# Selective scan: the read-out on TensorE one pair behind the scans instead of two, and the even step sizes issued at the end of the third pair

## The chip, the core and the metric

The kernel runs on one core of a Trainium2 chip. The metric is device time in microseconds (us) of one execution; the profile is one more execution, taken by the hardware profiler.

The core's engines work through their own instruction queues and meet at semaphores. The profile calls them PE (TensorE, matmuls; PEld are its weight loads), DVE (VectorE), ACT (ScalarE), POOL (GpSimd) and SP (SyncE). In this kernel SP issues all the DMAs that carry data.

## The reference

Two blocks run one after the other on an input of 16 images of 64 x 64 pixels with 96 channels. The first upsamples each image, passes it through a small network and downsamples it. The second holds the part that matters here, a selective scan along four directions over the 4096 pixels of an image, with 192 channels and 16 states for each direction:

```python
def selective_scan(u, dts, As, Bs, Cs, Ds, dt_bias):
    delta = jax.nn.softplus(dts + dt_bias[None, :, :, None])
    ...
    def step(h, inps):
        dt, ut, bt, ct = inps
        h = jnp.exp(dt[..., None] * As[None]) * h + (dt * ut)[..., None] * bt[:, :, None, :]
        y = jnp.einsum('bkdn,bkn->bkd', h, ct)
        return (h, y)
    _, ys = jax.lax.scan(step, h0, (dT, uT, BT, CT))
    ...
    return ys + u * Ds[None, :, :, None]
```

For each pixel the state `h` decays by `exp(delta * A)` and gains `delta * u * B`; the output `y` is the sum of `h * C` over the 16 states. Around this stand a normalization, an input projection, a depthwise convolution with silu, the projections that make `delta`, `B` and `C`, and an output projection.

## The kernel before

**Tiles.** A tile of the scan has 128 partitions: 32 channels times 4 states. A stretch of `T = 1024` pixels lies along the free axis. 16 states need four such tiles; the index `j` = 0 to 3 counts them. Two groups of 32 channels are taken together and are called the halves of a *pair*: the odd half, `e = 1`, and the even half, `e = 0`. Six blocks (`bi`) of two groups make up the 12 groups of 192 channels in two directions, and 128 steps (16 images, two direction pairs, four stretches) follow each other. So `units` lists 128 x 6 x 4 = 3072 pairs, numbered `n`, and `m = n // 4` counts the blocks.

**What a pair does.** `drive(n)` (L761, POOL) makes `delta * u * B` of both halves in one instruction, into a tile `b`. `decay(n, e)` (L755, ACT) makes `exp(delta * A)` of one half in PSUM, tile `da`. `recur(n, e)` (L770 forwards, L772 backwards, DVE) is the scan over the 1024 pixels; it overwrites `b` for the odd half and `da` for the even half (in every fifth pair `da` for both). The scan's result is multiplied by C: for the odd half on POOL (L917), for the even half on DVE (L927), both into `b`. In every fifth pair (`SHARE = 5`) the odd half's product is made on DVE too (L909). `keep` (L778) saves the last column of each scan for the next stretch. `read_out(n)` (L794, PE) sums the four states of each channel with eight matmuls (a quarter of the stretch of one half each) into the PSUM tile `y`, which gathers the four pairs of a block; for the second direction pair a matmul with `y0` (L787) opens the sum. `store` copies `y` out after a block's last pair (L805, ACT, tile `yt`) and sends it to HBM (L810 or L815, SP).

**Buffers.** There are four `b` tiles: `drive(n + 2)` writes where pair n - 2 was, so it waits for that pair's read-out. PSUM has two `da` tiles and one `y` tile. `delta` has three tiles in SBUF, each for one half of one block; `dtu`, the product of `delta` and `u`, has two. `bt` and `ct` have five tiles each.

**Order.** The order of the loop body is written by hand, and each engine keeps it. A pair n runs: fetches, odd scan, `keep`, `decay(n + 1, 1)`, `read_out(n - 2)`, slot 0, the odd product on POOL, `drive(n + 2)`, even scan, slot 1, even product, `keep`, `decay(n + 1, 0)`, slot 2, further fetches. The three *slots* are places where background work is put, a piece at a time: the projections of the next step (`project`, L655 to L696), the first block and convolution of the next image (`front`, L240 to L517) and the end of the last image (`finish`, L519 to L608). These share PE and ACT with the scan, and their pieces stand in the same queues.

**Fetches.** At `j == 0` SP issues the next block's `dtu`, at `j == 1` its odd `delta` and at `j == 3` its even `delta` (L703 issues all of them). `bt` and `ct` of the other direction are issued at the end of certain pairs (L722); in two of the six blocks that falls between pairs `j = 2` and `j = 3`. All of these carry 512 KB each.

Of the kernel before, what the change touches and what calls it, by code (L numbers as in the profile page):

```python
# [64 lines left out]
NQ = 4  # L65
# [14 lines left out]
def tile_two_blocks(  # L80
# [534 lines left out]
    def scan():  # L615


        with ExitStack() as es:
# [81 lines left out]
            def spread(out, what, ctx, bi, e):  # L700

                v, s0, r = blocks[bi]
                nc.sync.dma_start(  # L703
                    out=out,
                    in_=ctx[what][v][32 * (s0 + e):32 * (s0 + e) + 32, :].unsqueeze(1).to_broadcast([32, NQ, T]),
                )

            def fetch_dtu(ctx, bi):
                t = p2.tile([128, 2, T], F32, name="dtu")
                for e in range(2):  # L710
                    spread(t[:, e, :], "dtu", ctx, bi, e)
                return t

            def fetch_delta(ctx, bi, e):
                t = p3.tile([128, T], F32, name="delta")
                spread(t, "delta", ctx, bi, e)
                return t
# [16 lines left out]
            units = [(si_, bi, j) for si_ in range(len(steps)) for bi in range(len(blocks)) for j in range(NQ)]  # L734
# [7 lines left out]
            deltas = {(0, e): fetch_delta(ctxs[0], 0, e) for e in (1, 0)}  # L742
            y0s, states, ys = {}, [None] * len(blocks), {}

            def group(n, e):
                st, bi, _ = units[n]
                v, s0, r = blocks[bi]
                return 2 * steps[st][1] + r, s0 + e if v < 2 else 4 + e
# [3 lines left out]
            def decay(n, e):  # L752
                k, g = group(n, e)
                da = aps.tile([128, T], F32, name="da")
                nc.scalar.activation(da, deltas[n // NQ, e], AF.Exp, scale=a_s[:, k, g, units[n][2]:units[n][2] + 1])  # L755
                das[n, e] = da
# [23 lines left out]
            def read_out(n):  # L780
                st, bi, j = units[n]
                _, pair, lc = steps[st]
                if j == 0:
                    ys[n // NQ] = yps.tile([128, 2, QT], F32, name="y")
                y = ys[n // NQ]
                if j == 0 and pair == 1:
                    nc.tensor.matmul(  # L787
                        y.rearrange("p e t -> p (e t)"), lhsT=ident_s, rhs=y0s.pop((lc, bi)), start=True,
                        stop=False, skip_group_check=True,
                    )  # L790
                b = bs.pop(n)
                for e in range(2):
                    for q in range(NQ):
                        nc.tensor.matmul(  # L794
                            y[32 * q:32 * q + 32, e, :], lhsT=fold_s, rhs=b[:, e, QT * q:QT * q + QT],
                            start=(pair == 0 and j == 0 and e == 0), stop=(j == NQ - 1), skip_group_check=True,
                        )

            def store(n):

                st, bi, _ = units[n]
                mi, pair, lc = steps[st]
                v, s0, r = blocks[bi]
                yt = yp.tile([128, 2, QT], F32, name="yt")
                nc.scalar.copy(yt, ys.pop(n // NQ))  # L805
                yield
                if pair == 0:
                    part = dram.tile([128, 2 * QT], F32, name="part", tag=f"part{lc}_{bi}")
                    ypart[lc, bi] = part
                    nc.sync.dma_start(out=part, in_=yt.rearrange("p e t -> p (e t)"))  # L810
                else:
                    g = s0 if v < 2 else 4
                    for q in range(NQ):
                        first = T * lc + QT * q
                        nc.sync.dma_start(  # L815
                            out=image[mi]["y"][r, 32 * g:32 * g + 64, first:first + QT].rearrange(
                                "(e c) t -> c e t", e=2
                            ),
                            in_=yt[32 * q:32 * q + 32, :, :],
                        )  # L820

            class Background:
# [7 lines left out]
                def slot(self, position):  # L830
                    self.at += 1
                    if self.wait and position < 2:
                        return
                    if self.gen is not None and self.n * self.positions < self.at * self.slices:
                        self.step()
# [20 lines left out]
            last = len(units) - 1  # L856
# [13 lines left out]
            storing = None  # L870

            for n, (st, bi, j) in enumerate(units):
                mi, pair, lc = steps[st]
                v, s0, r = blocks[bi]
                m = n // NQ
                if n % per_image == 0:
                    image[mi]["y"] = dram.tile([2, DI, L], F32, name="y_d")
                    behind_gen.drain()
                    ahead_gen = behind_gen = nothing
                    if mi + 1 < B:  # L880
                        ahead_gen = Background(front(mi + 1), SLICES, POS)
                elif n % per_image == 2 and mi > 0:
                    behind_gen = Background(finish(mi - 1), SLICES, POS)
                if j == 0:
                    new = stp.tile([128, 2, NQ], F32, name="new", tag=f"st{bi}")
                    states[bi] = (states[bi][1] if states[bi] else None, new)

                if j == 0:
                    ahead = None
                    if bi + 1 < len(blocks):  # L890
                        ahead = ctxs[st], bi + 1
                    elif n + NQ <= last:
                        step_gen.drain()
                        ahead = ctxs[st + 1], 0
                        next_step(st + 2, mi)
                    if ahead:
                        dtus[m + 1] = fetch_dtu(*ahead)
                elif j == 1:
                    if ahead:
                        deltas[m + 1, 1] = fetch_delta(*ahead, 1)  # L900
                elif j == 3:
                    if ahead:
                        deltas[m + 1, 0] = fetch_delta(*ahead, 0)

                odd_here = n % SHARE == SHARE - 1
                h = das[n, 1] if odd_here else bs[n][:, 1, :]
                recur(n, 1, h)
                if odd_here:
                    nc.vector.tensor_mul(bs[n][:, 1, :], h, bc[1, r, j])  # L909
                keep(n, 1, h, nc.scalar.copy if odd_here else nc.vector.tensor_copy)  # L910
                if n < last:
                    decay(n + 1, 1)
                if n >= 2:
                    read_out(n - 2)
                slot(0)
                if not odd_here:
                    nc.gpsimd.tensor_mul(h, h, bc[1, r, j])  # L917
                if n + 2 <= last:
                    drive(n + 2)

                h = das[n, 0]
                recur(n, 0, h)
                if n >= 2 and units[n - 2][2] == NQ - 1:
                    storing = store(n - 2)
                    next(storing)
                slot(1)
                nc.vector.tensor_mul(bs[n][:, 0, :], h, bc[1, r, j])  # L927
                keep(n, 0, h, nc.scalar.copy)
                if n < last:
                    decay(n + 1, 0)  # L930
                slot(2)
                if storing is not None:
                    next(storing, 0)
                    storing = None
                if j == NQ - 1 and n < last and steps[units[n + 1][0]][1] == 1:
                    st2, bi2, _ = units[n + 1]
                    y0s[steps[st2][2], bi2] = fetch_y0(steps[st2][2], bi2)


                at = n % per_step  # L940
                for what in range(2):
                    ahead_j = at - (2 * NQ - 1 + what)
                    if 0 <= ahead_j < NQ:
                        bc[what, 1, ahead_j] = fetch_bc(ctxs[st], 1, ahead_j, what)
                    ahead_j = at - (5 * NQ - 1 + what)
                    if 0 <= ahead_j < NQ and st + 1 < len(steps):
                        bc[what, 0, ahead_j] = fetch_bc(ctxs[st + 1], 0, ahead_j, what)
            for n in (last - 1, last):
                read_out(n)
            for _ in store(last):  # L950
                pass
            behind_gen.drain()
# [109 lines left out]
```

## Time and profile before

| | us |
|---|---|
| median of 3 runs | 21647.74 |
| lowest and highest | 21629.93 and 21659.27 |
| the profiled execution | 21651.91 |
| its span, first to last instruction | 21650.1 |
| scan stage in it | 541 to 21488 |

A line of the groups gives: source line, engine, operation, tile written and read, shape, count, then busy time and mean duration of one in nanoseconds, then the idle time of the engine just before these instructions and what ended most of it. A line of the waits gives: who waited, for whom, us in total, number of times, longest. A timeline line gives the start in us, the length, engine, source line and operation, and in brackets the idle time before it.

The costliest instructions of the scan stage:

```profile
L761 POOL TENSOR_TENSOR b<-dtu,bt 128x2048 f32<-128x2048 f32 x3072 | 13898.6, 4531 | 1341.2 <-PE y L794 617.3
L755 ACT ACTIVATE da<-delta,a_s 128x1024 f32<-128x1024 f32 x6144 | 6845.6, 1116 | 3099.3 <-DVE b L770 795.3
L917 POOL TENSOR_TENSOR b<-b,ct 128x1024 f32<-128x1024 f32 x2458 | 5798.8, 2359 | 631.1 <-DVE new L778 291.2
L794 PE MATMUL y<-b,fold_s 128*32 128x256 f32 x49152 | 3623.5, 420 | 331.3 <-DVE b L927 141.1
L927 DVE TENSOR_TENSOR b<-da,ct 128x1024 f32<-128x1024 f32 x3072 | 3756.6, 1223 | 93.9
```

A scan takes about 2.3 us on DVE and there are two to a pair. Each fp32 matmul of the program stands in the trace as two.

### The profile page before, as it was taken

The page shows a single profiled execution, that of the slowest core. Times are in us where ns is not written, and L with a number is a line of the kernel's source. Part 1 is how long each engine was busy: PE and PEld are TensorE (multiplying, and loading weights), DVE is VectorE, ACT ScalarE, POOL GpSimd, SP SyncE. Part 2 cuts the span into 40 slices and gives each one's busy share as a digit, 9 for nine tenths or more (in the row PEclk, how much of TensorE's full clock was granted, in tenths as well). Part 3 has the DMA queues.
Part 4 walks back from the last instruction along what each step waited for, and adds up shares of the span by engine and source line. Part 5 has one row for each costly group of instructions (what it writes and reads, how often), then busy time and mean ns, then how long its engine had stood idle before and what let it go on. Part 6 is the DMA issues. An engine that isn't in the chain of part 4 may idle for free. (4 is left out here: it accounts for less than half of the span.)

```text
span 21650.1 us, 273738 instructions
## 1 busy us (share of the span) xinstructions
PE 16910.3 (78%) x98988; PEld 7341.1 (34%) x98988; DVE 19532.7 (90%) x12983; ACT 13726.8 (63%) x20546; POOL 19514.3 (90%) x5538
## 2 busy tenths in 40 slices
PE   7776877877778787887778788787787778877855
PEld 4423324233342333324333242333423333243221
DVE  0999999999999999999999999999999999999997
ACT  3666666666666666666666666676666666666553
POOL 0999999999999999999999999999999999999996
PEclk8887888988889888888888888888898888988977
DMA  2565565656656566565655656566565665656654
GB/s 71 182 206 183 201 220 185 222 188 204 217 184 224 185 216 200 191 226 180 219 194 201 221 183 215 192 204 213 191 226 182 214 201 193 225 181 219 216 188 141
DMA packets 1855467, 4277.13 MB, mean 198 GB/s; under 512 B 449438, under 2 KB 548670, under 8 KB 1852062
## 3 DMA queue, kind: packets, MB, share of 16 engines
q1 hardware_dynamic: 1854110, 4259.62, 59.0%
q8 instruction: 781, 12.80, 0.3%
q14 instruction: 576, 4.72, 0.1%
HBM read 3380.58 MB, written 878.18 MB: 197 GB/s over the span
## 5 line engine op out<-in xcount | busy, mean ns | idle before, releaser
L761 POOL TENSOR_TENSOR b<-dtu,bt 128x2048 f32<-128x2048 f32 x3072 | 13898.6, 4531 | 1341.2 <-PE y L794 617.3
L755 ACT ACTIVATE da<-delta,a_s 128x1024 f32<-128x1024 f32 x6144 | 6845.6, 1116 | 3099.3 <-DVE b L770 795.3
L917 POOL TENSOR_TENSOR b<-b,ct 128x1024 f32<-128x1024 f32 x2458 | 5798.8, 2359 | 631.1 <-DVE new L778 291.2
L794 PE MATMUL y<-b,fold_s 128*32 128x256 f32 x49152 | 3623.5, 420 | 331.3 <-DVE b L927 141.1
L927 DVE TENSOR_TENSOR b<-da,ct 128x1024 f32<-128x1024 f32 x3072 | 3756.6, 1223 | 93.9
L770 DVE TENSOR_TENSOR_SCAN da<-da,new,b 128x1024 f32<-128x1024 f32 x1383 | 3247.0, 2348 | 386.8 <-ACT da L755 361.7
L772 DVE TENSOR_TENSOR_SCAN da<-da,new,b 128x1024 f32<-128x1024 f32 x1382 | 3242.8, 2346 | 230.3 <-ACT da L755 212.4
L794 PEld LDWEIGHTS y<-b,fold_s 128*32 128x32 f32 x49152 | 1386.6, 117 | 2917.1 <-issue 1271.0
L686 PE MATMUL s<-w,ident_s 128*128 128x512 f32 x1536 | 1212.9, 882 | 1345.3 <-ACT w L681 1265.6
L772 DVE TENSOR_TENSOR_SCAN b<-da,new,b 128x1024 f32<-128x1024 f32 x922 | 2157.9, 2340 | 45.9 <-ACT da L755 36.3
L770 DVE TENSOR_TENSOR_SCAN b<-da,new,b 128x1024 f32<-128x1024 f32 x921 | 2156.3, 2341 | 13.3 <-ACT da L755 8.5
L778 ACT COPY new<-da 128x1 f32<-128x1 f32 x2764 | 434.6, 157 | 2723.5 <-DVE b L927 2195.3
L482 PE MATMUL c_ps<-xgp,wtap_s 96*128 96x512 f32 (+1 forms) x4608 | 1694.3, 635 | 163.2 <-ACT row L500 158.7
L666 PE MATMUL s<-pr,dtw_s 128*128 128x512 f32 x1536 | 1005.9, 741 | 1000.2 <-ACT pr L659 495.9
L365 PE MATMUL h_ps<-xu,w1t_s 96*128 96x500 f32 x1920 | 1044.0, 644 | 293.7 <-ACT hsq L348 120.6
L377 PE MATMUL o_ps<-w2c_s,hsq 128*100 128x96 f32 x9600 | 1061.3, 270 | 187.0 <-ACT hsq L348 161.8
L772 DVE TENSOR_TENSOR_SCAN da<-da,b 128x1024 f32<-128x1024 f32 x461 | 1055.9, 2291 | 120.4 <-ACT da L755 120.0
L770 DVE TENSOR_TENSOR_SCAN da<-da,b 128x1024 f32<-128x1024 f32 x460 | 1053.7, 2291 | 121.0 <-ACT da L755 116.5
L655 PE MATMUL pp<-u,xpt_s 128*128 128x512 f32 x1536 | 922.1, 741 | 305.7 <-DMA u<-xs_d 205.0
L377 PEld LDWEIGHTS o_ps<-w2c_s,hsq 128*100 128x100 f32 x9600 | 992.2, 182 | 393.0 <-ACT hsq L348 218.9
L686 PE MATMUL s<-e,ident_s 128*128 128x512 f32 x1536 | 1088.3, 800 | 0.0
L482 PEld LDWEIGHTS c_ps<-xgp,wtap_s 96*128 96x128 f32 (+1 forms) x4608 | 611.5, 173 | 1113.8 <-issue 896.3
(128 smaller groups left out, 21643.8 us busy)
## 6 DMA issues: line engine op xcount, KB each, us to landing
dtu<-dtu_d SPq DMA_DIRECT2D x1536, 512.0 KB
delta<-delta_d SPq DMA_DIRECT2D x1536, 512.0 KB
bt<-rows SPq DMA_DIRECT2D x1024, 512.0 KB
ct<-rows SPq DMA_DIRECT2D x1024, 512.0 KB
u<-xs_d SPq DMA_DIRECT2D x896, 256.0 KB
dtu_d<-dtu SPq DMA_DIRECT2D x768, 256.0 KB
delta_d<-delta SPq DMA_DIRECT2D x768, 256.0 KB
xr<-in_x SPq DMA_DIRECT2D x768, 128.0 KB
```

Of the source, the lines that this page charges most:

```text
L365: nc.tensor.matmul(h_ps[j], lhsT=w1t_s[:, 128 * j:128 * (j + 1)], rhs=xu.rearrange("c p q -> c (p q)"), start=True, stop=True,)
L377: nc.tensor.matmul(o_ps[:, p, :], lhsT=hsq[j][:, UPS * p:UPS * (p + 1)], rhs=w2c_s[:, j, :], start=(j == 0), stop=(j == HB - 1),)
L482: nc.tensor.matmul(c_ps[p:p + n], lhsT=wtap_s[:, tap, 128 * i:128 * i + n], rhs=xgp[:, h0:h0 + 8, dx:dx + HW], start=(tap == 0), stop=(tap ...
L666: nc.tensor.matmul(s, lhsT=dtw_s[:, pair, v, :], rhs=pr, start=True, stop=True)
L686: nc.tensor.matmul(s, lhsT=ident_s, rhs=of, start=(k == 0), stop=(k == 3))
L755: nc.scalar.activation(da, deltas[n // NQ, e], AF.Exp, scale=a_s[:, k, g, units[n][2]:units[n][2] + 1])
L761: nc.gpsimd.tensor_mul(b, dtus[n // NQ], bt.unsqueeze(1).to_broadcast([128, 2, T]))
L770: nc.vector.tensor_tensor_scan(out, da, b, before, ALU.mult, ALU.add)
L772: nc.vector.tensor_tensor_scan(out[:, ::-1], da[:, ::-1], b[:, ::-1], before, ALU.mult, ALU.add)
L794: nc.tensor.matmul(y[32 * q:32 * q + 32, e, :], lhsT=fold_s, rhs=b[:, e, QT * q:QT * q + QT], start=(pair == 0 and j == 0 and e == 0), sto ...
L917: nc.gpsimd.tensor_mul(h, h, bc[1, r, j])
L927: nc.vector.tensor_mul(bs[n][:, 0, :], h, bc[1, r, j])
```

## The change

It moves three things in the loop body, and nothing else:

```diff
-                elif j == 3:
-                    if ahead:
-                        deltas[m + 1, 0] = fetch_delta(*ahead, 0)
...
-                if n >= 2:
-                    read_out(n - 2)
                 slot(0)
+                if storing is not None:
+                    next(storing, 0)
+                    storing = None
...
                 recur(n, 0, h)
-                if n >= 2 and units[n - 2][2] == NQ - 1:
-                    storing = store(n - 2)
-                    next(storing)
+                if n >= 1:
+                    read_out(n - 1)
                 slot(1)
...
                     decay(n + 1, 0)
+                if n >= 1 and units[n - 1][2] == NQ - 1:
+                    storing = store(n - 1)
+                    next(storing)
                 slot(2)
-                if storing is not None:
-                    next(storing, 0)
-                    storing = None
+                if j == 2 and ahead:
+                    deltas[m + 1, 0] = fetch_delta(*ahead, 0)
...
-            for n in (last - 1, last):
-                read_out(n)
+            read_out(last)
```

The read-out of pair n - 1 now stands in pair n, behind the even scan and between slots 0 and 1; before, that of pair n - 2 stood in pair n ahead of slot 0. The first half of `store`, the copy of `y` on ACT, moves from between the even scan and slot 1 of the pair with `j = 1` to behind the even decay of the pair with `j = 0`. Its second half, the DMA, moves from behind slot 2 to behind slot 0, in the pair with `j = 1`. The even `delta` of the next block is issued behind slot 2 of pair `j = 2`, ahead of any `bt` and `ct` that are issued there, instead of at the start of pair `j = 3`. As two lines fall away above them, L909, L917 and L927 become L906, L915 and L924 in the changed program.

## What the change does to the time

> **What bounds the kernel now.** I read the page's busy shares first, then the busy time by stretch, the groups of VectorE by line with what ended their idle time, the waits of GpSimd, and the timeline at three stalls.
>
> ```profile
> PE 16910.3 (78%) x98988; PEld 7341.1 (34%) x98988; DVE 19532.7 (90%) x12983; ACT 13726.8 (63%) x20546; POOL 19514.3 (90%) x5538
> ...
> 541.00:21488.00 20947.00, 16368.15 (x96398) 7060.03 (x96398) 19504.72 (x12916) 13490.84 (x20168) 19511.11 (x5530) 0.86 0.60 202
> ```
>
> The second line is the scan stage: 20947 us for 3072 pairs, 6.82 us each. VectorE (DVE) works 19505 us of it and GpSimd (POOL) 19511 us, so both are near their floor and about 1440 us of idle time on each is all that a new order can win. Which wait ends last on DVE is told by its groups (busy, mean ns, idle before, releasers):
>
> ```profile
> L770 DVE TENSOR_TENSOR_SCAN da<-da,new,b 128x1024 f32<-128x1024 f32 x1383 | 3247.0, 2348 | 386.8 <-ACT da L755 361.7 <-POOL b L761 23.9
> L772 DVE TENSOR_TENSOR_SCAN da<-da,new,b 128x1024 f32<-128x1024 f32 x1382 | 3242.8, 2346 | 230.3 <-ACT da L755 212.4 <-POOL b L761 17.2
> ...
> L691 DVE TENSOR_TENSOR dtu<-s,u 128x512 f32<-128x512 f32 x768 | 523.5, 682 | 362.3 <-PE s L686 352.9 <-DMA out<-o 5.7 <-DMA dtu<-dtu_d 2.4
> ```
>
> Over all eight scan groups the decays of ACT (L755) end 993 us of DVE's idle time, GpSimd's drive (L761) only 58.6 us. L691 waits for TensorE 353 us, of which 156 (124 waits) lie in the scan stage. GpSimd's own waits look different:
>
> ```profile
> POOL b L761 <- PE y L794: 617.3, 365, 8.3
> ...
> POOL b L917 <- DVE new L778: 291.2, 224, 12.2
> ```
>
> 365 times a drive stands still until a read-out (L794) has released a `b` buffer. One such place, PE and then POOL:
>
> ```profile
> 11828.58 8.36 PE L482 MATMUL c_ps<-xgp,wtap_s 96*128 96x512 f32 x12 [4.66 <-ACT row L500]
> 11836.77 1.02 PE L686 MATMUL s<-w,ident_s 128*128 128x512 f32 x2
> ...
> 11841.16 1.07 PE L794 MATMUL y<-b,fold_s 128*32 128x256 f32 x16
> ```
>
> ```profile
> 11842.34 4.53 POOL L761 TENSOR_TENSOR b<-dtu,bt 128x2048 f32<-128x2048 f32 x1 [5.63 <-PE y L794]
> ```
>
> The read-out, 1.07 us of work whose data were ready, stands behind background matmuls of the pair before, and GpSimd idles 5.63 us. The two kinds of decay that make DVE wait are these:
>
> ```profile
> 10823.66 1.12 ACT L755 ACTIVATE da<-delta,a_s 128x1024 f32<-128x1024 f32 x1 [1.55 <-DVE b L772]
> ...
> 10824.81 2.36 DVE L772 TENSOR_TENSOR_SCAN da<-da,new,b 128x1024 f32<-128x1024 f32 x1 [1.00 <-ACT da L755]
> ```
>
> ```profile
> 8016.51 2.15 ACT L755 ACTIVATE da<-delta,a_s 128x1024 f32<-128x1024 f32 x2 [5.77 <-DMA delta<-delta_d]
> ```
>
> In the first, the even decay of a pair could start only when the odd scan of the same pair had emptied its PSUM tile; DVE then stands for 1.00 us. In the second, an even step size (`delta`) had not landed.
>
> **What the Trainium skill says.** "PSUM — Partial Sum Buffer", section "Engine vs sequencer instructions": ACT, VectorE and GpSimd take their queues strictly in order, and matmuls start and complete in program order. The timeline at 11836 agrees: a ready read-out waited for L686. "Perfetto Trace Analysis", section "Optimization Strategy": the same gap coming back can mean that the next tile finds no room in SBUF or PSUM; the 1.00 us gaps before even scans are of that kind. "DMA: Bandwidth & Descriptors", section "Queues, rings and completion order": a DMA engine takes its descriptors in ring order, so a transfer issued behind two others pays for them; the 5.77 us wait agrees. "SBUF — State Buffer", section "Who interferes with whom", has VectorE and GpSimd share a port pair as an exclusive lock; here L761 stays within 4482 to 4638 ns and L927 within 1199 to 1228, so I charge nothing when GpSimd's instructions shift in time.
>
> **The change part by part.** No instruction is added or removed, and the orders on DVE and POOL are the same in both programs, line by line. Only PE, ACT and SP queues are rearranged.
>
> *Read-out.* On PE the 8 matmuls of pair n-1 move ahead of the background of slots 1 and 2 of pair n and behind that of slot 0; on average they pass 5 matmuls. Going through the trace pair by pair, I took the end of the last matmul that stays ahead, added 1.1 us, and set it against the end of GpSimd's instruction before the drive that needs the buffer: of some 620 us of stalls about 12 us are left. The data are no obstacle: the odd half's product (L917) ended a median 3.3 us, and at the 99th percentile 0.0 us, before the even scan of the next pair began, and L927 at least 2.2 us before. So the GpSimd wait goes. Its worth for the end is not 617 us but what DVE lost: 58.6 us. Bounds 0 and -100 (scans set free may also let ACT go sooner); I take -55.
>
> *What is late next on PE.* One read-out more now lies in front of the work of slots 1 and 2. Where PE runs without a break that work comes 1.07 us later, and slot 0's as much sooner. L691 waits 124 times for L686 in the stage; some three fifths of these L686 groups lie in slots 1 and 2. Taking 75 x 1.07 = +80 us, less about 45 for the rest, gives +35; bounds -60 and 124 x 1.07 = +130. ACT's waits for PE (L310 378 us, L348 261 us as the largest) shift in the same way; as decays have about 1 us (even) or 2.4 us (odd) to spare, I take +20, bounds -20 and +100. PE itself waits for younger data in some pairs, but in 2404 pairs with passed work the first passed matmul would be later by 1611 us in sum, of which only 286 exceed the read-out's own 1.1 us.
>
> *Store.* The copy of `yt` (L805, 574 ns, 768 times) moves from in front of ACT's keep and even decay to behind that decay, where the next deadline is the odd decay's, with more room. It would find its read-out unfinished in 64 of 768 cases, 103 us in all, against 28.9 now. I take +15, bounds -40 and +75. Its DMA is issued about two slots sooner on SP; nothing there waits for it. TensorE's wait for `yt` before a block's first read-out is 846 us now and lies on PE's slack.
>
> *Even step sizes.* On SP the issue stays where it was in four of six blocks: end of pair 2 and start of pair 3 are the same place in the queue. In the two where `bt` and `ct` are fetched there, it passes both. ACT waits 369 us for `delta`; without the first load it is 127 waits and 280 us, all on the even half of a block's first pair, and 110 of them (231 us) in exactly those two blocks. DVE stood 138 us behind all, 111 us behind those. The issues take 0.65 us each, and 1 MB at 202 GB/s for a 0.60 share, so 337 GB/s at full share, is an estimated 3.1 us: up to 4.4 us sooner, against late times of up to 5.8. I take -85, bounds -20 (the ring was not the cause) and -111. `bt` and `ct` are later by one transfer and are needed two pairs afterwards.
>
> *PSUM tiles of the decay.* Which of the two tiles a decay gets depends on the order in which the program was laid out. By the semaphores, the even decay waits for the odd scan of its own pair in 550 pairs before and in 472 after (94 lost, 16 new). The 94 cost DVE 76 us in this trace; -76 + 16 x 1.0 = -60, bounds -80 and 0.
>
> Sum: -55 + 35 + 20 + 15 - 85 - 60 = -130 us. The profiled execution took 21651.9 us (span 21650.1), 4 us above the median of the runs. 21651.9 - 130 - 4 = 21518; I say 21520 us, 0.6% less.
>
> **The rivals.**
> - *GpSimd is the true bound* and its 617 us come back as time. For it: 90% busy, and in four of five pairs its 4.53 + 2.36 us exceed DVE's 5.9. Against: DVE waited for it 58.6 us only. Half of 617 with the other terms: 21651.9 - 4 - 309 - 75 = 21265, say 21300.
> - *Hidden or given back*: the decays of ACT stay the last wait, and what DVE gains it stands elsewhere. For it: 472 PSUM waits remain. Nearly all of -130 is lost: 21640.
> - *Slower*: PE in order. The read-out waits for a pair just finished, and the background behind it (projection, convolution) reaches ACT and DVE late. Price: the 1611 us of later matmul starts; from the point at which more than 200 us of that (one eighth) come through to scans, the gains are used up. At one fifth, 322 us: 21648 - 200 + 322 = 21770. Against: ACT reaches that work only after the odd scan and a decay, 2.34 + 1.12 = 3.5 us after L927.
> - *The fetch does nothing*, as the text of the change promises a pair and the queue shows two DMAs: 21520 + 85 = 21605; inside the forecast's own range.
>
> **How the numbers follow.** Forecast 0.64 (own range 21400 to 21604), GpSimd bound 0.12, hidden 0.12, slower 0.12. With all bounds good or bad the sum runs from -411 to +285 us; all at once is unlikely, so the range is 21370 to 21660, which leaves out most of the slow rival and of the GpSimd one. About 0.2%, 43 us, is what a measurement of this kernel can tell from no change: faster 0.76, same 0.12, slower 0.12.
>
> **What would show it.** GpSimd's L761 waits for PE below 60 us; DVE's for POOL below 15; ACT's waits for `delta` below 120 us; ACT's decays still ending some 850 us of DVE's idle time; L691's wait for L686 up by tens of us. I am wrong if the time falls by more than 250 us (then GpSimd was bound), or if L691, `row` or `hsq` wait hundreds of us more for TensorE.

## The result, and the profile after

| | before | after |
|---|---|---|
| median, us | 21646.94 | 21501.44 |
| lowest to highest | 21629.93 to 21659.27 | 21488.61 to 21508.85 |
| span of the profiled execution | 21650.1 | 21507.1 |
| scan stage in it | 543.0 to 21488.3 | 536.2 to 21343.3 |

The ratio is 0.9924, 95% interval 0.9912 to 0.9936: 145 us less. The scan stage gives 138 us of the span's 143. The scan stage is counted here from the first scan to the last product. The page's busy shares and the busy time of the scan stage (PE, PEld, DVE, ACT, POOL) show that no engine's work went away; the same work lies closer together:

```profile
PE 16918.9 (79%) x98988; PEld 7271.3 (34%) x98988; DVE 19512.2 (91%) x12983; ACT 13741.5 (64%) x20546; POOL 19511.8 (91%) x5538
...
536.00:21344.00 20808.00, 16384.12 (x96406) 6995.77 (x96410) 19484.51 (x12916) 13503.65 (x20167) 19506.86 (x5530) 0.86 0.60 203
```

The groups of VectorE, with what ended its idle time, answer to the three lines shown before:

```profile
L770 DVE TENSOR_TENSOR_SCAN da<-da,new,b 128x1024 f32<-128x1024 f32 x1383 | 3246.5, 2347 | 282.8 <-ACT da L755 274.7 <-POOL b L761 6.9
L772 DVE TENSOR_TENSOR_SCAN da<-da,new,b 128x1024 f32<-128x1024 f32 x1382 | 3242.4, 2346 | 125.5 <-ACT da L755 119.1 <-POOL b L761 5.2
...
L691 DVE TENSOR_TENSOR dtu<-s,u 128x512 f32<-128x512 f32 x768 | 523.5, 682 | 431.9 <-PE s L686 430.6 <-DMA delta<-delta_d 0.8
```

The two largest groups lost 209 us of idle time, and L691's wait for TensorE grew by 78 us. Over all eight scan groups the waits for GpSimd fell from 58.6 to 22.7 us. GpSimd's own waits, and ACT's for `delta` without the program's first load (350 us in 140 waits before):

```profile
POOL b L915 <- DVE new L778: 832.6, 438, 16.0
...
POOL b L761 <- PE y L794: 47.9, 25, 5.3
```

```profile
ACT da L755 <- DMA delta<-delta_d: 60.3, 19, 4.5
```

GpSimd hardly waits for read-outs any more (617.3 us before); it waits for VectorE instead (291.2 us before). Its idle time mostly changed hands: in the scan stage it shrank from 1436 us to 1301, no more than the stage did. The place that stalled it in the timeline of before looks like this after, first TensorE, then VectorE, then GpSimd:

```profile
11756.75 1.07 PE L794 MATMUL y<-b,fold_s 128*32 128x256 f32 x16
11757.75 2.84 PE L482 MATMUL c_ps<-xgp,wtap_s 96*128 96x512 f32 x6
11760.43 1.02 PE L686 MATMUL s<-w,ident_s 128*128 128x512 f32 x2
```

```profile
11764.06 0.69 DVE L691 TENSOR_TENSOR dtu<-s,u 128x512 f32<-128x512 f32 x1 [3.55 <-PE s L686]
```

```profile
11758.43 4.51 POOL L761 TENSOR_TENSOR b<-dtu,bt 128x2048 f32<-128x2048 f32 x1
```

In the trace of before the same L691 stood like this:

```profile
11840.41 0.69 DVE L691 TENSOR_TENSOR dtu<-s,u 128x512 f32<-128x512 f32 x1 [1.42 <-PE s L686]
```

The read-out now precedes the background, and the drive starts without a wait (5.63 us before). The background pays: L691, which waited 1.42 us there, waits 3.55.

To see the whole of it I went through VectorE's instructions in both traces, and put each idle stretch over 0.05 us in the scan stage down to the operand that came last. An even decay counts as "own tile" when the program makes it wait for the odd scan of its own pair (in every fifth pair for the product that follows it). The first row has those that began within 0.15 us of that release, 435 before and 419 after. The second has 101 and 58 whose tile had been free for longer when ACT, busy with other work, came to them; the tile did not hold these up. The rows are good to some 3 us.

| VectorE idle, us | before | after | two tags, before (E3) | two tags, after (E4) |
|---|---|---|---|---|
| even decay, own tile, begun at its release | 392 | 378 | 0 | 0 |
| even decay, own tile, but ACT later still | 165 | 82 | 0 | 0 |
| even decay, `delta` not landed | 139 | 38 | 187 | 34 |
| even decay, late otherwise | 38 | 23 | 224 | 136 |
| odd decay late | 209 | 304 | 184 | 223 |
| L691 for TensorE | 160 | 232 | 176 | 157 |
| drive (GpSimd) | 56 | 16 | 66 | 24 |

So the even decays that ACT made late, whatever their tile (second and fourth row), cost 203 us before and 105 after, while the tile itself cost nearly as much as before.

### The profile page after: what moved, and what is told of

Its sections match the earlier page's. It is cut to its first block, busy times and chain, and to the rows that moved or that the text cites. A ratio compares the mean times of both kernels' runs of the same rounds, so it can differ in the third digit from the quotient of the medians.

```text
span 21507.1 us, 273615 instructions
## 1 busy us (share of the span) xinstructions
PE 16918.9 (79%) x98988; PEld 7271.3 (34%) x98988; DVE 19512.2 (91%) x12983; ACT 13741.5 (64%) x20546; POOL 19511.8 (91%) x5538
## 5 line engine op out<-in xcount | busy, mean ns | idle before, releaser
L915 POOL TENSOR_TENSOR b<-b,ct 128x1024 f32<-128x1024 f32 x2458 | 5804.1, 2361 | 1235.6 <-DVE new L778 832.6
L794 PE MATMUL y<-b,fold_s 128*32 128x256 f32 x49152 | 3837.1, 435 | 1111.6 <-DVE b L924 551.4
L924 DVE TENSOR_TENSOR b<-da,ct 128x1024 f32<-128x1024 f32 x3072 | 3756.5, 1223 | 93.9
L666 PE MATMUL s<-pr,dtw_s 128*128 128x512 f32 x1536 | 939.0, 696 | 544.6 <-ACT delta L692 328.0
L686 PE MATMUL s<-e,ident_s 128*128 128x512 f32 x1536 | 1022.9, 755 | 0.0
L787 PE MATMUL y<-y,ident_s 128*128 128x512 f32 x768 | 534.1, 784 | 538.6 <-ACT yt L805 537.1
```

Source lines behind the costliest of these rows:

```text
L666: nc.tensor.matmul(s, lhsT=dtw_s[:, pair, v, :], rhs=pr, start=True, stop=True)
L686: nc.tensor.matmul(s, lhsT=ident_s, rhs=of, start=(k == 0), stop=(k == 3))
L794: nc.tensor.matmul(y[32 * q:32 * q + 32, e, :], lhsT=fold_s, rhs=b[:, e, QT * q:QT * q + QT], start=(pair == 0 and j == 0 and e == 0), sto ...
```

## The experiments

Each ratio is that of a kernel's runs to those of the kernel before taken beside them, with its 95% interval. Differences in us are those of the medians; taken from the ratios they would be up to some 30 us smaller or larger.

**E1, the fetch alone.** To the kernel before:

```diff
-                elif j == 3:
-                    if ahead:
-                        deltas[m + 1, 0] = fetch_delta(*ahead, 0)
...
+                if j == 2 and ahead:
+                    deltas[m + 1, 0] = fetch_delta(*ahead, 0)
```

> The kernel before with only the even step sizes issued at the end of pair j = 2; read-out and store stay where they were. My theory: this part alone frees VectorE of about 85 to 100 us of waits, so about 21555 us, ratio 0.996; ACT's waits for delta fall from 369 us to below 120, and GpSimd still waits some 600 us for read-outs. Even decays that wait for their own pair's odd scan: 556 by the program, 550 before, so no gain from there. Rival (the transfer is hidden anyway, or only two places in SP's queue are not enough): 21620 to 21650 us, ratio 0.999 to 1.000.

Measured: 21586.55 us, ratio 0.9970 (0.9962 to 0.9979), so about 65 us, of the 85 to 100 expected. ACT's waits for `delta` fell from 369.1 to 106.6 us, and VectorE's idle time behind them from 139 to 31 us. Of these 108 us, 22 came back as own-tile waits (579 us in this program, with its 556 decays of that kind) and 26 at L691. On the first pairs of the two blocks whose fetch passes `bt` and `ct`, ACT's waits fell from 290 us to 32 (first load left out); on those of block 5, whose place in the queue is unchanged, they stayed (47 and 49 us). The fetch works through two places in a queue; the rival falls. In these two blocks the issue itself also came 1.0 to 1.3 us sooner (medians), and how much is due to that and how much to the order of the transfers was not separated.

**E2, read-out and store alone.** The change without the lines of E1.

> The changed kernel with the even step sizes put back to the start of pair j = 3: read-out and store alone. My theory: GpSimd's waits for read-outs fall from 617 us to about 50, which is worth about 40 us to VectorE; 462 instead of 550 even decays wait for their own pair's odd scan, worth about 90; background matmuls that come later cost 60 to 100. Sum -50 us: 21600 us, ratio 0.9975. Rival (GpSimd is the true bound): all of the change's 145 us and more come from here, 21500 us or below, ratio 0.993.

Measured: 21578.74 us, ratio 0.9970 (0.9960 to 0.9981). GpSimd's waits for read-outs are 44.1 us as foreseen, but VectorE gained only 41 us from that. Its 462 own-tile decays cost 425 us, 133 less than before, but only some 53 us of that are decays that began at the tile's release (392 to 339); the rest are decays that ACT reached sooner (165 to 81). Odd decays (+98) and L691 (+59) take back more than the read-out gave. So in this kernel the read-out's own aim is worth no more than each of these side effects. No run changes the tile assignment alone.

**E3 and E4, a PSUM tile of its own for each half.** To the kernel before and to the changed one:

```diff
-            aps = es.enter_context(tc.tile_pool(name="sc_aps", bufs=2, space=PSUM))
+            aps = es.enter_context(tc.tile_pool(name="sc_aps", bufs=1, space=PSUM))
...
-                da = aps.tile([128, T], F32, name="da")
+                da = aps.tile([128, T], F32, name="da", tag=f"da{e}")
```

> The kernel before, but each half's decay has a PSUM tile of its own (two tags of one tile instead of two tiles that either half may take). No even decay can then wait for its own pair's odd scan. My theory: VectorE's 557 us of waits behind those 550 decays are true losses; most of them come back, 300 to 500 us: 21150 to 21350 us, ratio 0.977 to 0.986. Rival (ACT is late anyway, and what goes here is given back at the next wait): less than 100 us, 21550 us or more, ratio above 0.995.

> The changed kernel with the same two tags. My theory: 458 us of VectorE's waits go, 250 to 420 us come back: 21080 to 21250 us, ratio 0.974 to 0.982. The distance to the kernel before with two tags is then what the change is worth without its gain in PSUM tiles: 40 to 80 us, if the sum of the prediction holds without its term of 60. Rival (GpSimd bound): with VectorE set free the read-out's place decides, and the distance between the two is over 150 us. Rival (hidden): this is within 100 us of the changed kernel.

Measured: 21278.54 us, ratio 0.9834 (0.9821 to 0.9848), and 20955.87 us, ratio 0.9685 (0.9671 to 0.9698). The same PSUM memory in two tags is worth 376 us to the kernel before and 546 to the changed one (359 and 517 by the ratios). To the kernel before that is nearly the 392 us of decays that began at the tile's release. To the changed one it is more than its 378, and more than I expected: odd decays (-81) and L691 (-75) wait less too. TensorE's granted clock also rose in these kernels, from 0.857 to 0.864 (E3) and from 0.856 to 0.870 (E4), and its busy time for the same matmuls fell by 132 and 263 us; what part of the gain that made was not tried. The distance between E3 and E4 is 323 us where I expected 40 to 80, which is what the GpSimd rival had said. The groups of VectorE in E3 and then in E4 show that its mechanism is not the cause:

```profile
L772 DVE TENSOR_TENSOR_SCAN da<-da,new,b 128x1024 f32<-128x1024 f32 x1382 | 3242.4, 2346 | 202.5 <-ACT da L755 185.5 <-POOL b L761 15.8
```

```profile
L772 DVE TENSOR_TENSOR_SCAN da<-da,new,b 128x1024 f32<-128x1024 f32 x1382 | 3241.7, 2346 | 52.1 <-ACT da L755 44.9 <-POOL b L761 6.0
```

The decay, not the drive, makes most of the difference. By the table, 153 us of it are step sizes that land late, 88 are even decays that ACT made late, and 42 are GpSimd. With the own-tile stalls gone from the kernel before, the even decays that ACT makes late stayed near where they were (203 to 224 us), and those whose `delta` has not landed cost more (139 to 187).

**E5 and E6, the two parts under two tags.**

> Two tags for the decay, and of the change the even step sizes alone. In the runs with two tags the whole change was worth about 320 us, more than twice what it is worth without them. Theory A (the faster loop leaves a transfer less time, so the late step sizes cost more: 187 us of VectorE's waits before, 34 after): this part alone is worth 110 to 160 us: 21120 to 21170 us. Theory B (GpSimd's read-out waits became the bound): it is worth less than 70 us: above 21210 us.

> Two tags for the decay, and of the change the read-out and the store without the step sizes. Theory A: 100 to 190 us, so 21090 to 21180 us; VectorE's waits for GpSimd fall by about 40 us only and its waits for even decays that ACT makes late by about 90. Theory B: 250 us and more, below 21030 us.

Measured: 21133.23 us, ratio 0.9756 (0.9742 to 0.9771), and 21131.24 us, ratio 0.9757 (0.9742 to 0.9772). Against E3 each part is worth about 146 us (some 168 by the ratios), and both together 323. Theory A's numbers hold, Theory B's do not: in E5 only the `delta` waits moved down by more than a few us (187 to 22), in E6 the late even decays (224 to 135), the drive (66 to 21) and, by 24 us, `delta`, while odd decays rose by 55 us.

**E7, the copy of `y` ahead of the even decay.** To E4:

```diff
                 slot(1)
+                if n >= 1 and units[n - 1][2] == NQ - 1:
+                    storing = store(n - 1)
+                    next(storing)
                 nc.vector.tensor_mul(bs[n][:, 0, :], h, bc[1, r, j])
...
                     decay(n + 1, 0)
-                if n >= 1 and units[n - 1][2] == NQ - 1:
-                    storing = store(n - 1)
-                    next(storing)
```

> Two tags and the whole change, but the copy of y on ACT stands directly behind slot 1 of pair j = 0, in front of the even product, of keep and of the even decay, instead of behind that decay. Theory (the copy in front of the even decay is what made even decays late): VectorE's waits for late even decays rise from 136 us towards 224, ACT's waits for the read-out rise over 35 us, time 50 to 150 us more than with the copy behind: 21000 to 21100 us. Rival (the copy's place is worth nothing, the read-out's own place did it): within 25 us of 20956 us.

Measured: 21046.27 us, ratio 0.9717 (0.9701 to 0.9733), 90 us more than E4. Late even decays are at 238 us, and ACT waits for the read-out:

```profile
ACT yt L805 <- PE y L794: 421.7, 228, 6.7
```

So the copy of `y` behind the even decay, a part of the change that I had counted as a small cost, is worth about 90 us under two tags against this place. It is not that of before, which was one pair later, where ACT waited 31.5 us for the read-out (E3): part of the 90 us is the wait for the read-out, so they don't price the move that the change makes.

**E8, more work for GpSimd.** To E4: `SHARE = 6`.

> Two tags and the whole change, with SHARE = 6: every sixth pair instead of every fifth has its odd product on VectorE. That takes 102 products of 1.22 us from VectorE (125 us) and gives 102 of 2.36 us to GpSimd (241 us). Theory (VectorE's chain sets the time, and GpSimd has over 500 us of waits for it): 40 to 125 us faster, 20830 to 20915 us. Rival (GpSimd is the bound): slower than 20956 us, by up to 240 us.

Measured: 21055.01 us, ratio 0.9722 (0.9707 to 0.9736), 99 us more than E4: my theory fails here. VectorE's waits for the drive rise from 24 to 93 us and those for late odd decays from 222 to 274, and of the 125 us of products taken from VectorE nothing is left in its busy time (19463.2 against 19462.9 us), mostly because a tiny multiply took longer:

```profile
L236 DVE TENSOR_TENSOR nb<-nmean,rg 96x1 f32<-96x1 f32 x32 | 234.9, 7339 | 319.0 <-ACT rg L233 319.0
```

In E4 it is busy 131.6 us with a mean of 4113 ns. GpSimd is busy 94% of this run (93% in E4), and the work that it took over came back to VectorE as waits and in this multiply.

**E9, the read-out behind slot 1.** To E4:

```diff
-                if n >= 1:
-                    read_out(n - 1)
                 slot(1)
+                if n >= 1:
+                    read_out(n - 1)
```

> Two tags and the whole change, with the read-out of pair n - 1 behind slot 1 instead of ahead of it. Theory (one more read-out ahead of the background costs VectorE a little through L686 and L691, and GpSimd's freedom is bought with it): VectorE's wait of L691 for L686 falls from 160 us to 120 to 150, GpSimd's waits for read-outs rise from 25 us to 80 to 250, and the two nearly cancel: 20920 to 21010 us. Rival (the read-out's exact place is what the change lives on): over 21050 us.

Measured: 21271.37 us, ratio 0.9823 (0.9807 to 0.9840), 315 us more than E4. My theory fails, and the rival's number came in. GpSimd's waits, 205.5 us, lie where I expected them and cost VectorE only 5 us more, but L691's wait rose to 215.8 us instead of falling. The largest part is ACT, which comes to the copy of `y` too soon:

```profile
ACT yt L805 <- PE y L794: 356.9, 216, 7.3
```

Late odd decays rise from 223 to 324 us (those directly behind the copy from 65 to 195) and late even ones from 136 to 225. By this trace the copy behind the read-out, more than the drive, limits how late the read-out may stand; the copy was not moved along with it to try this.

**E10, the tiny multiply on ACT.** To E4:

```diff
-        nc.vector.tensor_mul(nb, nmean, rg)
+        nc.scalar.activation(nb, nmean, AF.Identity, scale=rg)
```

> Two tags and the whole change, with the product of nmean and rg (96 x 1, L236, 32 times, both operands in SBUF) made by ACT instead of VectorE. On VectorE it takes 4.1 us on average and ends when an instruction of GpSimd ends. Theory (VectorE is locked out by GpSimd there, and stands): VectorE gains the 132 us that L236 takes and most of 14 us of waits: 100 to 145 us, 20810 to 20860 us. Rival (the time is given back at the next wait for ACT or GpSimd): less than 40 us, above 20915 us.

Measured: 20895.02 us, ratio 0.9645 (0.9631 to 0.9659), the fastest kernel of this study. 61 us of at most 145 come back (87 by the ratios), between the two expectations. L691's wait took 33 of the rest (157 to 190 us), and another small multiply with both operands in SBUF took 24 (L259, 96 x 96, 16 times: busy 13.6 us in E4, 38.0 here).

## Why the prediction was right

The forecast was 21520 us, the measured time 21501. The direction and the two aims of the change were right in mechanism. That the sum came so near is partly luck: several terms were off by some 35 us and the errors cancelled, and what I could put down to terms comes to some -120 of the stage's -138 us. Of what was to be seen, GpSimd's 47.9 us for read-outs, ACT's 60.3 us for `delta` and 865 us of VectorE's idle time ended by decays (850 foreseen, over the eight scan groups) came out.

- *Read-out to GpSimd, -55.* Right in mechanism and nearly in size: about -40. The 617 us of GpSimd's waits were never on the path as such; E2 shows them gone for 41 us of VectorE's time. Left are 22.7 us by the groups, where I expected under 15.
- *L691 later, +35.* The direction was right, the size double: 78 us by the groups, inside its bounds. Sorted by the slot in which L691 stands, those of slot 0 gave back 39 us (72 to 33), near the 45 that I had let them; those of slots 1 and 2 lost 110 (88 to 198) where I had 80.
- *Other background, +20, and store, +15.* Together about nothing, from two large parts: odd decays +95, even decays that ACT made late -98 (203 to 105). Some 68 us of the odd ones lie behind the copy of `yt`, where that of before had 3. The copy's own wait for the read-out, for which I had 103 us, is 34.6. The gain on even decays comes with the read-out and the store (E2 has it, and E6 against E3); how it divides between the copy's place and the read-out's is open.
- *Even step sizes, -85.* Measured -101 in the trace, and E1 gives 65 us of time for it alone. The place behind `bt` and `ct` was the cause. My reading of the waits was low: without the first load the trace has 350 us in 140 waits, not 280 in 127, and 290 us of them in the two blocks, not 231.
- *PSUM tiles, -60.* The conflicts that went and came are as forecast: the pairs of the 94 lost cost 76 us before and 5 after, those of the 16 new none before and 15 after. On the pairs that stayed, decays that had been late for another reason came to wait for the tile instead, and those begun at its release rose from 316 to 363 us. So the row of such decays fell by 14 us only (392 to 378).
- *Nothing for collisions of VectorE and GpSimd* was not quite true: L236 and its waits are 32 us less (160.8 to 145.6 busy, 31 to 14 waiting).

Of the rivals, *GpSimd is the true bound* is refuted for these two kernels by E2 and by the table; E8 shows that under two tags more work for GpSimd costs time. *Hidden or given back* describes E1, where 65 of 108 us arrived. *Slower* had its mechanism right, since background behind the read-out does come later, at some 160 us of waits at most (L691 and odd decays) and not the 322 it needed. Of the change's 145 us, E1 and E2 give 65 each; the 15 us between their sum and the whole are within the intervals.

That the copy's place matters so much (E7, E9) was not in the prediction.

## What to carry to other kernels

The idle time of an engine that is near its floor is worth only what the chain behind it waited: price a stall at its consumer. Two kinds of tile that rotate through one pool can be assigned so that one waits for the other; a regular gap of the length of one producer is the sign, and a tag for each kind, at no cost in memory, gave 376 us here. A wait that the program has is not always the wait that came last: of the own-tile decays before, 101 with 165 us were late for another reason. A change can be worth twice as much once another stall is gone (323 us against 145 here), so its parts are to be measured again after each large gain.

## What the runs showed of the hardware

A VectorE multiply of 96 x 1 elements with both operands in SBUF took 0.155 us at its shortest and 12.2 us at its longest (L236). In the trace of after, VectorE and then GpSimd:

```profile
3781.38 12.03 DVE L236 TENSOR_TENSOR nb<-nmean,rg 96x1 f32<-96x1 f32 x1
```

```profile
3782.13 2.35 POOL L915 TENSOR_TENSOR b<-b,ct 128x1024 f32<-128x1024 f32 x1
3784.43 8.96 POOL L761 TENSOR_TENSOR b<-dtu,bt 128x2048 f32<-128x2048 f32 x2
```

It ends at 3793.41, with the last of three GpSimd instructions at 3793.39. Of the 32, in each of the two traces 30 took over 0.3 us and ended within 0.03 us after the end of a GpSimd instruction. An addition of the same 96 x 1 with one operand in PSUM (L258, 16 times) never took more than 0.155 us. This agrees with the exclusive lock of the Trainium skill's "SBUF — State Buffer", section "Who interferes with whom", which the prediction named and looked for in the wrong instructions: the scans and L927 take one of their two large operands from PSUM and never waited, as their steady durations show (2.27 to 2.36 us and 1.20 to 1.23 us). In the lines above VectorE also stayed out while GpSimd passed from one instruction to the next. Moving the 32 to ACT, where each took at most 0.3 us, was worth 61 us (E10).
